# A graph-attention layer with a resident mask: eleven exponential tiles, the mask in nine pieces, the second mask quarter made before the main loop

## The chip, the cores and the metric

The kernel runs on one core of a Trainium2 chip. The metric is the device time of one execution in microseconds (us), the median of three runs. The core has a matrix engine (TensorE, PE in the profile; its weight loads are PEld), a vector engine (DVE), a scalar engine (ACT), GpSimd (POOL), a sync engine (SP) that here only issues transfers, and 16 DMA engines.

## The reference, cut to what matters

`x` is (8, 2048, 256) float32, `adj` is (2048, 2048) int32, one adjacency for all eight samples f. Heads: 8 of 32 channels.

```python
qkv = jnp.einsum('fnc,ck->fnk', x, w_qkv)
q, k, v = jnp.split(qkv, 3, axis=-1)            # then 8 heads of 32 channels
scores = jnp.einsum('fnhd,fmhd->fhnm', q, k) / jnp.sqrt(D)
scores = jnp.where((adj > 0)[None, None], scores, -1e9)
attn = jax.nn.softmax(scores, axis=-1)
t = jnp.einsum('fhnm,fmhd->fnhd', attn, v).reshape(F, N, C)
x = layernorm(x + t); x = layernorm(x + mlp(x)); x = layernorm(x0 + x)
```

## The kernel before

The 2048 queries of a sample are cut into four chunks `qc` of 512, the heads into two halves `g` of four heads, the keys into 16 blocks `mb` of 128. One **item** is (f, qc, g, mb); there are 8·4·2·16 = 1024 of them. The 16 items of one (f, qc, g) are called a **group** here and are numbered from 0 to 63, so that f = 0 is groups 0 to 7. An item makes scores for four heads (PE), adds the mask (DVE, two halves of 1024 columns), takes the exponential in place (ACT) and multiplies by V (PE). The sum of the exponentials is gathered in three chains, two by accumulating DMA and one on POOL, and finished by a matmul with ones (`denominator`).

The tiles that the change touches: `pp` holds the exponential tiles (8 KB a partition each), `mkp` the mask of one query chunk (16 blocks of 512 fp8 values, 8 KB a partition).

```python
mkp = ctx.enter_context(tc.tile_pool(name="mkp", bufs=2))
ld = ctx.enter_context(tc.tile_pool(name="ld", bufs=LD))          # LD = 3
pp = ctx.enter_context(tc.tile_pool(name="pp", bufs=10))
# ...
def scores(item):
    f, qc, g, mb = item
    pt = PT[item] = pp.tile([P, 4, CH], F32, name="p")
    ps2 = [score_pair() for _ in range(2)]
    # ... 4 matmuls into the two PSUM pairs (L223)
    for half, ps in enumerate(ps2):
        nc.vector.tensor_tensor(pt[:, 2 * half:2 * half + 2, :], ps,
                                MK[f, qc][:, mb, None, :].to_broadcast([P, 2, CH]), ALU.add)      # L226
    nc.scalar.activation(pt, pt, AF.Exp, scale=1.0 / math.sqrt(D))                                # L228

POOLED = (0, 3, 6, 8, 11, 13, 15)
MOVED = ((1, 4, 7, 10), (2, 5, 9, 12))
ALONE = 14

def add_up(item):
    f, qc, g, mb = item
    for chain in MOVED:
        if mb in chain[1:]:
            nc.gpsimd.dma_start(PT[f, qc, g, chain[0]], PT.pop(item), accum_op=ALU.add)           # L257
    if mb in POOLED[1:]:
        first = PT[f, qc, g, POOLED[0]]
        nc.gpsimd.tensor_tensor(first, first, PT.pop(item), ALU.add)                              # L260
```

A mask quarter is the mask of one query chunk. It is made once, during f = 0, from `adj`: a load, a conversion on DVE, 16 transposes of 128x128 per 512 keys on PE, and two copies out of PSUM on DVE. It is then stored in DRAM (`MD`) and loaded again for every other sample.

```python
def turn_mask(qc, mc):
    if mc == 0:
        MK[0, qc] = mkp.tile([P, MB, CH], F8, name="mask")
    yield INPUTS - 3
    cv = take([P, TPC, CH], BF16)
    ts = [take([P, 2, CH], I32) for _ in range(2)]
    for half, t in enumerate(ts):
        q0 = qc * CH + half * 2 * P
        nc.sync.dma_start(t, adj[q0:q0 + 2 * P, ...])                                             # L121
        nc.vector.tensor_scalar(cv[:, ...], t, 0.0, MASKED, op0=ALU.is_le, op1=ALU.mult)          # L122
        give(t)
        yield 1
    yield 1
    yield from mask_blocks(qc, mc, cv)      # transposes L136, copies L137; whole quarter stored, L140
    give(cv)

def load_mask(f, qc):
    MK[f, qc] = mkp.tile([P, MB, CH], F8, name="mask")
    nc.sync.dma_start(words(MK[f, qc]), MD[qc])                                                   # L144
```

`begin` runs before the main loop. It loads x and the adjacency of chunk 0 into the exponential tiles, makes K, V of the first head half and mask quarter 0, issues the scores of the first two items, and then makes K, V of the second head half:

```python
def begin():
    # ... loads, L427 and L428
    for c in range(NCK):
        nc.vector.tensor_scalar(cv[c], cols[c], 0.0, MASKED, op0=ALU.is_le, op1=ALU.mult)         # L431
        # ... turn rows, queries, project(0, c, 0)
        yield from mask_blocks(0, c, cv[c])
    for k in range(LEAD):                                                                         # LEAD = 2
        scores(items[k])
    for c in range(NCK):
        yield from project(0, c, 1, rows[c][:, 2:4, :])
```

The main loop walks the items in order. Everything else (masks, queries, projections of the next sample, the layer norms and the MLP, called the tail) stands in a list `fill`, sorted by due item; a `yield n` in it means that the next step is taken n items later at the earliest, and a step that needs a PSUM bank takes the one bank that each item has to spare.

```python
for t, (f, qc, g, mb) in enumerate(items):
    if f == 0 and g == 0 and mb == 0 and qc + 1 < NCK:
        start(t, mask_ahead(qc + 1), t + 28)
    if g == 1 and mb == 0 and (f or qc == NCK - 1) and (f + 1 < F or qc + 1 < NCK):
        load_mask(f + (qc + 1) // NCK, (qc + 1) % NCK)
    # ... work for the next sample is put into the list
    if mb:
        advance(t, 1)
    scores(items[t + LEAD])     # (cut: waits here until V of that item is made)
    values(items[t]); add_up(items[t])
    if mb == LAST:
        start(t + SUM, denominator(f, qc, g), t)
```

Of the kernel before, what the change touches and what calls it, by code (L numbers as in the profile page):

```python
# [30 lines left out]
MASKED = -57344.0  # L31
# [22 lines left out]
def fast_path(ctx, tc, cst, x, adj, out, RS):  # L54
    nc = tc.nc
    F, N, C = x.shape
    NCK, TPC, MB = N // CH, CH // P, N // P

    LD = 3
    dp = ctx.enter_context(tc.tile_pool(name="dp", bufs=1, space=bass.MemoryType.DRAM))  # L60
    mkp = ctx.enter_context(tc.tile_pool(name="mkp", bufs=2))
    ld = ctx.enter_context(tc.tile_pool(name="ld", bufs=LD))
    kp = ctx.enter_context(tc.tile_pool(name="kp", bufs=2 * NCK + 2))
    qp = ctx.enter_context(tc.tile_pool(name="qp", bufs=2 * NCK + 2))
    vp = ctx.enter_context(tc.tile_pool(name="vp", bufs=2 * NCK + 2))
    pp = ctx.enter_context(tc.tile_pool(name="pp", bufs=10))
    work = ctx.enter_context(tc.tile_pool(name="work", bufs=1))
    yp = ctx.enter_context(tc.tile_pool(name="yp", bufs=2))
    op = ctx.enter_context(tc.tile_pool(name="op", bufs=1))
# [28 lines left out]
    def take(shape, dt):  # L98
        live.pop(0)
        live.append(ld.tile(shape, dt, name="in"))  # L100
        return live[-1]

    def give(t):
        live[:] = [None if u is t else u for u in live]


    MD = dp.tile([NCK, P, MB * CH // 4], I32, name="md")
    MK = {}

    def words(mask):  # L110
        return mask.rearrange("p b q -> p (b q)").bitcast(I32)

    def turn_mask(qc, mc):
        if mc == 0:
            MK[0, qc] = mkp.tile([P, MB, CH], F8, name="mask")
        yield INPUTS - 3
        cv = take([P, TPC, CH], BF16)
        ts = [take([P, 2, CH], I32) for _ in range(2)]
        for half, t in enumerate(ts):
            q0 = qc * CH + half * 2 * P  # L120
            nc.sync.dma_start(t, adj[q0:q0 + 2 * P, mc * CH:(mc + 1) * CH].rearrange("(j p) m -> p j m", p=P))  # L121
            nc.vector.tensor_scalar(cv[:, 2 * half:2 * half + 2, :], t, 0.0, MASKED, op0=ALU.is_le, op1=ALU.mult)  # L122
            give(t)
            yield 1
        yield 1
        yield from mask_blocks(qc, mc, cv)
        give(cv)

    def mask_blocks(qc, mc, cv):
        for half in range(2):  # L130
            yield BANK
            ps = bank(BF16)
            for r in range(2):
                for j in range(TPC):
                    rr = 2 * half + r
                    nc.tensor.transpose(ps[:, r, j * P:(j + 1) * P], cv[:, j, rr * P:(rr + 1) * P], identb)  # L136
            nc.vector.tensor_tensor(MK[0, qc][:, mc * TPC + 2 * half:mc * TPC + 2 * half + 2, :], ps,  # L137
                                    cst["ones"][:, 0:1, None].to_broadcast([P, 2, CH]), ALU.min, saturate=False)
        if mc == NCK - 1:
            nc.sync.dma_start(MD[qc], words(MK[0, qc]))  # L140

    def load_mask(f, qc):
        MK[f, qc] = mkp.tile([P, MB, CH], F8, name="mask")
        nc.sync.dma_start(words(MK[f, qc]), MD[qc])  # L144


    QT, KT, V, XT = {}, {}, {}, {}
# [37 lines left out]
    def reload(f, c):  # L185
        while (f, c) not in XT:
            yield 1
        yield INPUTS - 1
        xT = take([P, 2, CH], F32)
        nc.sync.dma_start(xT, XD[f][c])  # L190
        yield 3
        return xT

    def project(f, c, g, xT=None):
        if xT is None:
            xT = yield from reload(f, c)
            while len(KT) < (2 * f + g) * NCK + c:
                yield 1
        yield BANK
        KT[f, c, g] = channels(kp, "kT", xT, C + g * P)  # L200
        yield BANK
        ps = bank()
        for j in range(TPC):
            for a in range(2):
                nc.tensor.matmul(ps[:, j * P:(j + 1) * P], xT[:, a, j * P:(j + 1) * P],  # L205
                                 wqkv[:, a, 2 * C + g * P:2 * C + (g + 1) * P], start=(a == 0), stop=(a == 1))
        v = vp.tile([P, TPC, P], F32, name="v")
        nc.scalar.copy(v, ps.rearrange("p (j c) -> p j c", c=P))
        V[f, c, g] = v
        give(xT)  # L210
# [9 lines left out]
        for half in (1, 0):  # L220
            for j in range(2):
                r = D * (2 * half + j)
                nc.tensor.matmul(ps2[half][:, j, :], KT[f, mb // TPC, g][r:r + D, (mb % TPC) * P:(mb % TPC + 1) * P],  # L223
                                 QT[f, qc, g][r:r + D, :], start=True, stop=True)
        for half, ps in enumerate(ps2):
            nc.vector.tensor_tensor(pt[:, 2 * half:2 * half + 2, :], ps,  # L226
                                    MK[f, qc][:, mb, None, :].to_broadcast([P, 2, CH]), ALU.add)
        nc.scalar.activation(pt, pt, AF.Exp, scale=1.0 / math.sqrt(D))  # L228

    LAST = MB - 1  # L230
# [149 lines left out]
    def start(t, gen, due):  # L380
        fill.append([t, gen, 1, due])
        fill.sort(key=lambda e: e[3])
# [24 lines left out]
    def mask_ahead(qc):  # L407
        for mc in range(NCK):
            yield from turn_mask(qc, mc)
# [9 lines left out]
    def begin():  # L419
        flat = [pp.tile([P, 4, CH], F32, name="p").rearrange("p a q -> p (a q)") for _ in range(NCK + NCK // 2)]  # L420
        cols = [t.bitcast(I32).rearrange("p (j m) -> p j m", m=CH) for t in flat[:NCK]]
        cv = [t[:, i * 2 * CH:(i + 1) * 2 * CH].bitcast(BF16).rearrange("p (j m) -> p j m", m=CH)
              for t in flat[NCK:] for i in range(2)]
        rows = [pp.tile([P, 4, CH], F32, name="p") for _ in range(NCK)]
        for c in range(NCK):
            xc = rows[c][:, 0:2, :].rearrange("p a (b c) -> p (a b) c", c=C)
            nc.sync.dma_start(xc, x[0, c * CH:(c + 1) * CH, :].rearrange("(j p) c -> p j c", p=P))  # L427
            nc.sync.dma_start(cols[c], adj[0:CH, c * CH:(c + 1) * CH].rearrange("(j p) m -> p j m", p=P))  # L428
        MK[0, 0] = mkp.tile([P, MB, CH], F8, name="mask")
        for c in range(NCK):  # L430
            nc.vector.tensor_scalar(cv[c], cols[c], 0.0, MASKED, op0=ALU.is_le, op1=ALU.mult)  # L431
            xT = rows[c][:, 2:4, :]
            yield from turn_rows(rows[c][:, 0:2, :].rearrange("p a (b c) -> p (a b) c", c=C), xT)
            nc.sync.dma_start(XD[0][c], xT)
            XT[0, c] = xT
            if c == 0:
                yield from queries(0, 0, xT)
            yield from project(0, c, 0, xT)
            yield from mask_blocks(0, c, cv[c])
        for k in range(LEAD):  # L440
            scores(items[k])
        for c in range(NCK):
            yield from project(0, c, 1, rows[c][:, 2:4, :])

    def ask(f, c):
        xT = yield from reload(f, c)
        yield from queries(f, c, xT)
        give(xT)

    for _ in begin():  # L450
        pass
    for c in range(1, NCK):
        start(0, ask(0, c), 2 * MB * c - LEAD - 1)
    state["side"] = 0
    for t, (f, qc, g, mb) in enumerate(items):
        if mb == 0 and t:
            state["side"] = 1 - state["side"]
        if f == 0 and g == 0 and mb == 0 and qc + 1 < NCK:
            start(t, mask_ahead(qc + 1), t + 28)
        if g == 1 and mb == 0 and (f or qc == NCK - 1) and (f + 1 < F or qc + 1 < NCK):  # L460
            load_mask(f + (qc + 1) // NCK, (qc + 1) % NCK)
        if f + 1 < F:
            for what, *which in NEXT.get((2 * qc + g, mb), []):
                due = t + MB // 2 if what is turn else items.index((f + 1, 0, which[1], which[0] * TPC)) - LEAD - 1
                start(t, what(f + 1, *which), due)
        if mb:
            advance(t, 1)
        if t + LEAD < len(items):
            nf, _, ng, nmb = items[t + LEAD]
            t0 = t  # L470
            while (nf, nmb // TPC, ng) not in V:
                advance(t0, 1)
                t0 += 1
            scores(items[t + LEAD])
        values(items[t])
        add_up(items[t])
        if mb == LAST:
            start(t + SUM, denominator(f, qc, g), t)
    t = len(items)
# [239 lines left out]
```

## Time and profile before

| what | value |
|---|---|
| time, median of 3 | 3736.42 us (3731.55 to 3740.82) |
| profiled span | 3732.1 us, mean granted TensorE clock 0.977 |
| busy: PE, DVE, POOL, ACT | 3241.8, 2760.8, 2599.1, 2411.0 us |
| mean DMA traffic | 154 GB/s, 573.31 MB |
| mask loads from DRAM | 28 of 1024 KB, 6.6 us to landing |

The page counts an engine as busy while an instruction of the program runs on it. A row of the groups names the line, the engine and the operation, then what it writes and reads, the count, the busy time and the mean duration, and the idle time of that engine just before such instructions with what ended it. In the list of waits a row "A <- B: s, n, m" says that A sat idle for B for s us in total, n times, m us at the longest. In a timeline a number in brackets is idle time just before the instruction. With 1024 items, an average item takes 3.6 us.

### The profile page before, as it was taken

What the parts mean: (1) busy time and instruction counts of PE and PEld (TensorE: products, weight loads), DVE (VectorE), ACT (ScalarE), POOL (GpSimd) and SP (SyncE); (2) the same over time, 40 slices, a digit from 0 to 9 for tenths busy, and PEclk for the clock granted to TensorE, in tenths of its full rate; (3) what the DMA queues carried; (4) which work ended last, traced back from release to release, by engine and by line L of the source; (5) the groups of instructions that cost most, each with busy time, mean ns of one, the idle gap of its engine ahead of it and who ended that gap; (6) DMA issues with size and microseconds to landing.
All of it is one profiled execution on the core that took longest, in us unless ns stands there. A gap on an engine that the chain in (4) does not pass through costs nothing. (4 is left out here: it accounts for less than half of the span.)

```text
span 3732.1 us, 53786 instructions
## 1 busy us (share of the span) xinstructions
PE 3241.8 (87%) x22020; PEld 1038.8 (28%) x22020; DVE 2760.8 (74%) x3203; ACT 2411.0 (65%) x1921; POOL 2599.1 (70%) x1363
## 2 busy tenths in 40 slices
PE   7877888899988899889998899889898889988884
PEld 4222223222322233222332223222232222322221
DVE  4777766877688766788677777777768877688883
ACT  3554555766667666766666776666666676677663
POOL 2555666777677775877667785777777777687775
PEclk9998999999999999999999999999999999999997
DMA  6766675776766775776766776676676676676664
GB/s 185 175 142 152 146 175 117 168 162 142 173 150 145 158 171 145 169 153 154 169 138 151 163 172 158 140 165 154 147 175 141 148 171 152 154 164 140 139 134 86
DMA packets 113774, 573.31 MB, mean 154 GB/s; under 512 B 10833, under 2 KB 27729, under 8 KB 60273
## 3 DMA queue, kind: packets, MB, share of 16 engines
q0 software_dynamic: 64848, 436.90, 58.1%
q1 hardware_dynamic: 47856, 131.61, 10.0%
q8 instruction: 174, 2.85, 0.3%
q10 hardware_dynamic: 816, 1.31, 0.1%
q14 instruction: 80, 0.65, 0.0%
HBM read 129.37 MB, written 37.75 MB: 45 GB/s over the span
## 5 line engine op out<-in xcount | busy, mean ns | idle before, releaser
L226 DVE TENSOR_TENSOR p<-s,mask 128x1024 f32<-128x1024 f32 x2048 | 2410.3, 1219 | 753.8 <-PE s L223 480.0
L228 ACT ACTIVATE p<-p 128x2048 f32<-128x2048 f32 x1024 | 1957.1, 1911 | 1232.9 <-DVE p L226 916.2
L260 POOL TENSOR_TENSOR p<-p 128x2048 f32<-128x2048 f32 x384 | 1835.9, 4810 | 653.6 <-ACT p L228 645.0
L223 PE MATMUL s<-qT,kT 32*128 32x512 f32 x8192 | 1193.2, 652 | 232.5 <-DVE p L226 231.0
L240 PE MATMUL x<-p,v 128*32 128x512 f32 x8192 | 1112.2, 616 | 0.0
L257 POOL DMA_DIRECT2D p<-p x384 | 382.7, 1018 | 351.2 <-ACT p L228 138.9
L223 PEld LDWEIGHTS s<-qT,kT 32*128 32x128 f32 x8192 | 325.3, 186 | 853.6 <-DVE p L226 695.6
L240 PEld LDWEIGHTS x<-p,v 128*32 128x32 f32 x8192 | 162.3, 108 | 795.2 <-issue 645.1
L180 PE MATMUL x<-in,wqkv 128*128 128x512 f32 x472 | 234.6, 620 | 23.1 <-ACT oT L244 10.2
L278 ACT ACTIVATE y<-y,nb,rs 128x256 f32<-128x256 f32 x384 | 224.9, 589 | 38.0 <-POOL nb L275 38.0
L294 PE MATMUL x<-p,ones 128*32 128x512 f32 x2048 | 246.3, 599 | 1.8 <-DVE y L364 0.9
L267 DVE BATCH_NORM_STATS2 st<-y 128x6 f32<-128x256 f32 x384 | 160.1, 417 | 27.1 <-DMA y<-in_x_dram 27.1
L362 PE MATMUL x<-w2s,hT 128*128 128x256 f32 x512 | 127.6, 392 | 45.7 <-ACT oT L244 42.3
L352 PE MATMUL x<-turned,w1s 128*128 128x512 f32 x256 | 128.8, 626 | 20.8 <-ACT hT L353 19.5
L180 PEld LDWEIGHTS x<-in,wqkv 128*128 128x128 f32 x472 | 80.3, 190 | 186.1 <-issue 69.8
L362 PEld LDWEIGHTS x<-w2s,hT 128*128 128x128 f32 x512 | 92.1, 190 | 112.0 <-ACT oT L244 68.6
L205 PE MATMUL x<-wqkv,in 128*128 128x128 f32 x896 | 114.9, 282 | 6.4 <-ACT kT L182 6.3
L205 PEld LDWEIGHTS x<-wqkv,in 128*128 128x128 f32 x896 | 104.2, 192 | 55.0 <-ACT kT L182 34.0
L364 DVE TENSOR_TENSOR y<-x,y 128x512 f32<-128x512 f32 x64 | 44.3, 692 | 94.9 <-PE x L362 94.7
L294 PEld LDWEIGHTS x<-p,ones 128*32 128x32 f32 x2048 | 64.0, 111 | 165.8 <-issue 129.7
L272 POOL TENSOR_TENSOR rs<-rs,mhalf 128x4 f32<-128x4 f32 x96 | 99.3, 1035 | 8.0
L341 PE MATMUL x<-ident,y 128*128 128x128 f32 x256 | 48.0, 299 | 54.5 <-ACT turned L342 38.8
(87 smaller groups left out, 1427.1 us busy)
## 6 DMA issues: line engine op xcount, KB each, us to landing
p<-p POOLq DMA_DIRECT2D x384, 1024.0 KB, 9.7
y<-in_x_dram POOLq DMA_DIRECT2D x64, 512.0 KB, 6.1
in<-xd SPq DMA_DIRECT2D x59, 512.0 KB, 8.0
mask<-md SPq DMA_DIRECT2D x28, 1024.0 KB, 6.6
out_dram<-y SPq DMA_DIRECT2D x32, 512.0 KB, 3.0
in<-in_x_dram SPq DMA_DIRECT2D x28, 512.0 KB, 6.9
xd<-in SPq DMA_DIRECT2D x28, 512.0 KB, 10.0
in<-in_adj_dram SPq DMA_DIRECT2D x24, 512.0 KB, 7.6
```

The source lines that it names most:

```text
L180: nc.tensor.matmul(ps, wqkv[:, a, k0:k0 + P], xT[:, a, :], start=(a == 0), stop=(a == 1))
L205: nc.tensor.matmul(ps[:, j * P:(j + 1) * P], xT[:, a, j * P:(j + 1) * P], wqkv[:, a, 2 * C + g * P:2 * C + (g + 1) * P], start=(a == 0), s ...
L223: nc.tensor.matmul(ps2[half][:, j, :], KT[f, mb // TPC, g][r:r + D, (mb % TPC) * P:(mb % TPC + 1) * P], QT[f, qc, g][r:r + D, :], start=Tr ...
L226: nc.vector.tensor_tensor(pt[:, 2 * half:2 * half + 2, :], ps, MK[f, qc][:, mb, None, :].to_broadcast([P, 2, CH]), ALU.add)
L228: nc.scalar.activation(pt, pt, AF.Exp, scale=1.0 / math.sqrt(D))
L240: nc.tensor.matmul(O[grp][r:r + D, :], V[f, mb // TPC, g][:, mb % TPC, r:r + D], PT[item][:, h, :], start=(mb == 0), stop=(mb == LAST))
L257: nc.gpsimd.dma_start(PT[f, qc, g, chain[0]], PT.pop(item), accum_op=ALU.add)
L260: nc.gpsimd.tensor_tensor(first, first, PT.pop(item), ALU.add)
L267: nc.vector.bn_stats(st, t[:, j, :])
L278: nc.scalar.activation(t[:, j, :], t[:, j, :], AF.Identity, bias=nb[:, j:j + 1], scale=rs[:, j:j + 1])
L294: nc.tensor.matmul(ps[r:r + D, :], cst["ones"], term[:, h, :], start=(n == 0), stop=(n == 3))
L362: nc.tensor.matmul(ps[:, (j - jj) * C:(j - jj + 1) * C], hT[:, d, j * P:(j + 1) * P], w2s[:, d, :], start=(d == 0), stop=(d == 1))
```

## The change

The two whole mask buffers (16 KB a partition) become nine pieces of two key blocks (1 KB each, 9 KB together); the room goes to an eleventh exponential tile. A sample's mask is loaded piece by piece: while the second head half of one query chunk runs, at every second item one piece of the next chunk's mask is loaded, each as soon as it has been made. During f = 0 the quarters 1 to 3 are also loaded back from DRAM instead of being built in place: what the copies out of PSUM write is a staging place in the load buffers, and from there it is stored. The two loads and the two conversions of a step of `turn_mask` are set apart by two items. Mask quarter 1 is made in `begin`, beside K and V of the second head half, with exponential tiles as load buffers; quarters 2 and 3 start at items 16 and 32.

```diff
-    mkp = ctx.enter_context(tc.tile_pool(name="mkp", bufs=2))
+    mkp = ctx.enter_context(tc.tile_pool(name="mkp", bufs=MB // 2 + 1))
-    pp = ctx.enter_context(tc.tile_pool(name="pp", bufs=10))
+    pp = ctx.enter_context(tc.tile_pool(name="pp", bufs=11))
...
     def turn_mask(qc, mc):
-        if mc == 0:
-            MK[0, qc] = mkp.tile([P, MB, CH], F8, name="mask")
         yield INPUTS - 3
...
             nc.sync.dma_start(t, adj[q0:q0 + 2 * P, mc * CH:(mc + 1) * CH].rearrange("(j p) m -> p j m", p=P))
+        yield 2
+        for half, t in enumerate(ts):
             nc.vector.tensor_scalar(cv[:, 2 * half:2 * half + 2, :], t, 0.0, MASKED, op0=ALU.is_le, op1=ALU.mult)
-            give(t)
-            yield 1
-        yield 1
-        yield from mask_blocks(qc, mc, cv)
+        yield 1
+        yield from mask_blocks(qc, mc, cv, [... the two load buffers, seen as fp8 ...])
+        for t in ts:
+            give(t)
         give(cv)
...
-            nc.vector.tensor_tensor(MK[0, qc][:, ...], ps, ..., ALU.min, saturate=False)
-        if mc == NCK - 1:
-            nc.sync.dma_start(MD[qc], words(MK[0, qc]))
+            k = 2 * mc + half
+            m = to[half] if to else mask_piece(0, qc, k)
+            nc.vector.tensor_tensor(m, ps, ..., ALU.min, saturate=False)
+            nc.sync.dma_start(MD[qc, k], words(m))
+            made.add((qc, k))
-    def load_mask(f, qc):
-        MK[f, qc] = mkp.tile([P, MB, CH], F8, name="mask")
-        nc.sync.dma_start(words(MK[f, qc]), MD[qc])
+    def load_mask(f, qc, k):
+        nc.sync.dma_start(words(mask_piece(f, qc, k)), MD[qc, k])
...
         for c in range(NCK):                                    # in begin
+            t = pp.tile([P, 4, CH], F32, name="p").rearrange("p a q -> p (a q)")
+            col = t.bitcast(I32).rearrange("p (j m) -> p j m", m=CH)
+            nc.sync.dma_start(col, adj[CH:2 * CH, c * CH:(c + 1) * CH].rearrange("(j p) m -> p j m", p=P))
+            nc.vector.tensor_scalar(cv[c], col, 0.0, MASKED, op0=ALU.is_le, op1=ALU.mult)
             yield from project(0, c, 1, rows[c][:, 2:4, :])
+            yield from mask_blocks(1, c, cv[c], [... two parts of t, seen as fp8 ...])
...
     for c in range(1, NCK):
         start(0, ask(0, c), 2 * MB * c - LEAD - 1)
+        if c > 1:
+            start(MB * (c - 1), mask_ahead(c), 2 * MB * c - MB // 2)
...
-        if f == 0 and g == 0 and mb == 0 and qc + 1 < NCK:
-            start(t, mask_ahead(qc + 1), t + 28)
-        if g == 1 and mb == 0 and (f or qc == NCK - 1) and (f + 1 < F or qc + 1 < NCK):
-            load_mask(f + (qc + 1) // NCK, (qc + 1) % NCK)
+        if g == 1 and mb % 2 and (f + 1 < F or qc + 1 < NCK):
+            coming.append((f + (qc + 1) // NCK, (qc + 1) % NCK, mb // 2))
+        while coming and coming[0][1:] in made:
+            load_mask(*coming.popleft())
```

More of the change, by code (lines that the diff above doesn't have):

```diff
@@ L104, in give, with mask_piece @@
         live[:] = [None if u is t else u for u in live]
-    MD = dp.tile([NCK, P, MB * CH // 4], I32, name="md")
+    MD = dp.tile([NCK, MB // 2, P, 2 * CH // 4], I32, name="md")
     MK = {}
+    made, coming = set(), deque()
     def words(mask):
         return mask.rearrange("p b q -> p (b q)").bitcast(I32)
+    def mask_piece(t, qc, k):
+        MK[t, qc, k] = mkp.tile([P, 2, CH], F8, name="mask")
+        return MK[t, qc, k]
     def turn_mask(qc, mc):
-        if mc == 0:
-            MK[0, qc] = mkp.tile([P, MB, CH], F8, name="mask")
         yield INPUTS - 3
@@ L121, in turn_mask, with mask_blocks @@
             nc.sync.dma_start(t, adj[q0:q0 + 2 * P, mc * CH:(mc + 1) * CH].rearrange("(j p) m -> p j m", p=P))
+        yield 2
+        for half, t in enumerate(ts):
             nc.vector.tensor_scalar(cv[:, 2 * half:2 * half + 2, :], t, 0.0, MASKED, op0=ALU.is_le, op1=ALU.mult)
+        yield 1
+        yield from mask_blocks(qc, mc, cv, [t.rearrange("p j m -> p (j m)").bitcast(F8)[:, 0:2 * CH].rearrange("p (b q) -> p b q", q=CH)
+                                            for t in ts])
+        for t in ts:
             give(t)
-            yield 1
-        yield 1
-        yield from mask_blocks(qc, mc, cv)
         give(cv)
-    def mask_blocks(qc, mc, cv):
+    def mask_blocks(qc, mc, cv, to=None):
         for half in range(2):
@@ L136, in mask_blocks @@
                     nc.tensor.transpose(ps[:, r, j * P:(j + 1) * P], cv[:, j, rr * P:(rr + 1) * P], identb)
-            nc.vector.tensor_tensor(MK[0, qc][:, mc * TPC + 2 * half:mc * TPC + 2 * half + 2, :], ps,
-                                    cst["ones"][:, 0:1, None].to_broadcast([P, 2, CH]), ALU.min, saturate=False)
-        if mc == NCK - 1:
-            nc.sync.dma_start(MD[qc], words(MK[0, qc]))
-    def load_mask(f, qc):
-        MK[f, qc] = mkp.tile([P, MB, CH], F8, name="mask")
-        nc.sync.dma_start(words(MK[f, qc]), MD[qc])
+            k = 2 * mc + half
+            m = to[half] if to else mask_piece(0, qc, k)
+            nc.vector.tensor_tensor(m, ps, cst["ones"][:, 0:1, None].to_broadcast([P, 2, CH]), ALU.min, saturate=False)
+            nc.sync.dma_start(MD[qc, k], words(m))
+            made.add((qc, k))
+    def load_mask(f, qc, k):
+        nc.sync.dma_start(words(mask_piece(f, qc, k)), MD[qc, k])
     QT, KT, V, XT = {}, {}, {}, {}
@@ L226, in scores @@
             nc.vector.tensor_tensor(pt[:, 2 * half:2 * half + 2, :], ps,
-                                    MK[f, qc][:, mb, None, :].to_broadcast([P, 2, CH]), ALU.add)
+                                    MK[f, qc, mb // 2][:, mb % 2, None, :].to_broadcast([P, 2, CH]), ALU.add)
         nc.scalar.activation(pt, pt, AF.Exp, scale=1.0 / math.sqrt(D))
@@ L428, in begin @@
             nc.sync.dma_start(cols[c], adj[0:CH, c * CH:(c + 1) * CH].rearrange("(j p) m -> p j m", p=P))
-        MK[0, 0] = mkp.tile([P, MB, CH], F8, name="mask")
         for c in range(NCK):
@@ L442, in begin @@
         for c in range(NCK):
+            t = pp.tile([P, 4, CH], F32, name="p").rearrange("p a q -> p (a q)")
+            col = t.bitcast(I32).rearrange("p (j m) -> p j m", m=CH)
+            nc.sync.dma_start(col, adj[CH:2 * CH, c * CH:(c + 1) * CH].rearrange("(j p) m -> p j m", p=P))
+            nc.vector.tensor_scalar(cv[c], col, 0.0, MASKED, op0=ALU.is_le, op1=ALU.mult)
             yield from project(0, c, 1, rows[c][:, 2:4, :])
+            yield from mask_blocks(1, c, cv[c], [t[:, i * CH // 2:(i + 1) * CH // 2].bitcast(F8).rearrange("p (b q) -> p b q", q=CH)
+                                                 for i in range(2)])
     def ask(f, c):
```

## The prediction

> **What bounds the kernel now.** I read the page's busy table first.
>
> ```profile
> PE 3241.8 (87%) x22020; PEld 1038.8 (28%) x22020; DVE 2760.8 (74%) x3203; ACT 2411.0 (65%) x1921; POOL 2599.1 (70%) x1363
> ```
>
> TensorE is busy for 87% of the span and nothing else comes near. The change removes no score, value or projection, so it can win only idle time of PE: 3732 - 3242 = 490 us at the very most. Where does it lie? I cut the span at the first value matmul of each sample (start of the loop at 58 us, its end at 3664) and asked for the table by stage. Columns: window, its length, busy PE, PEld, DVE, ACT, POOL, then clock, DMA share, GB/s.
>
> ```profile
> 0.00:58.00 58.00, 47.13 (x292) 31.83 (x296) 19.32 (x18) 19.82 (x29) 6.75 (x19) 1.00 0.64 215
> 58.00:568.00 510.00, 412.36 (x2760) 125.96 (x2756) 378.40 (x391) 282.59 (x207) 297.87 (x135) 0.93 0.67 154
> 568.00:1031.00 463.00, 414.52 (x2804) 137.33 (x2800) 336.80 (x395) 306.37 (x253) 325.53 (x172) 0.99 0.70 157
> 1031.00:1474.00 443.00, 396.96 (x2716) 126.45 (x2712) 335.62 (x392) 300.53 (x240) 323.98 (x168) 1.00 0.71 157
> ```
>
> Sample 0, which makes the masks, takes 510 us with 98 of them idle on PE; sample 1 takes 463; sample 2 and the four after it 443 to 448, with some 46 idle. Sample 0 is thus 65 us, sample 1 about 18 us longer than a settled one. The 18 sit in its first group alone, 69 us against 52 in a later sample:
>
> ```profile
> 568.00:637.00 69.00, 60.35 (x408) 24.00 (x404) 42.93 (x51) 39.69 (x36) 42.12 (x24) 0.98 0.67 153
> 1474.00:1526.00 52.00, 44.66 (x332) 13.63 (x324) 42.71 (x49) 34.51 (x24) 32.10 (x18) 0.98 0.65 135
> ```
>
> PE has 16 us more work there: projections for which sample 0 found no free bank in time. So the masks cost time where they are made, and again as a backlog.
>
> Then the waits of DVE that the change touches, in the list of waits:
>
> ```profile
> DVE in L122 <- DMA in<-in_adj_dram: 35.6, 8, 8.6
> ...
> DVE p L226 <- DMA p<-p: 25.8, 19, 5.0
> ```
>
> The first is the adjacency load that is issued and converted in one step. The timeline at 280 us shows what one costs: issued at 280.45, converted at 283.16, and PE stood still for 7.23 us, because the scores' PSUM pairs were not emptied:
>
> ```profile
> 283.16 0.69 DVE L122 TENSOR_SCALAR in<-in 128x1024 bf16<-128x1024 int32 x1 [8.64 <-DMA in<-in_adj_dram]
> ...
> 285.04 2.09 PE L223 MATMUL s<-qT,kT 32*128 32x512 f32 x8 [7.23 <-DVE p L226]
> ```
>
> The matmuls after it took 2.09 us for 1.14, so a stop costs a little more than its length. The second wait is the exponential tile: all ten are taken, and the next is free only when an accumulating DMA has read it. Seen at 1523 us, in the second item of a group:
>
> ```profile
> 1522.93 2.36 DVE L226 TENSOR_TENSOR p<-s,mask 128x1024 f32<-128x1024 f32 x2 [1.46 <-DMA p<-p]
> ```
>
> **What the Trainium skill says.** "SBUF — State Buffer", section "SBUF: two separate sides": DVE and GpSimd share one port pair as an exclusive lock, so one blocks for the whole of the other's instruction. The trace agrees: a conversion (L122) has a median of 0.685 us and took 5.56 us at 214.72, while a POOL addition ran from 214.93 for 4.80 us. Before the loop POOL does no such additions; conversions moved there are safe. "DMA: Bandwidth & Descriptors", section "Anatomy of one DMA — SWDGE (gpsimd) path": a wait sits on the issuing sequencer before dispatch, so transfers that one engine issues stand in a line. The trace agrees: SP spends 1736 us in total at the xT store (L171) until ACT has made xT, and what it issues later stands behind that. "Perfetto Trace Analysis", section "DMA Optimizations": transfers under 2 KB carry a large overhead. This would speak against 1 KB pieces, but the packets of the hardware queue in this trace took 50 ns for 1 KB and 365 for 8 KB, the same per byte; the measurement decides, and I charge the pieces nothing.
>
> **Part 1, eleven tiles.** In the built program the tile taken by the second item of a group is that of the item 7 before (the tenth of the last group, end of a DMA chain); with eleven tiles it is that of the item 8 before. Put against the times of this trace, the new previous users would be done at least 2.7 us before their tile is wanted in samples 1 to 7 (the old ones: 0.1 us, and late in 23 cases). So the wait goes. Of the 25.8 us about 5 lie in one stop in sample 0; from 568 us on there are 19.3 us in 17 waits. A stopped item takes 4.0 to 4.4 us where an unstopped one in the same place takes 2.83, and the next sometimes 0.7 more: 15 stops of weight at 1.2 to 1.9 us is 18 to 28. I take **-22**.
>
> **Part 2, conversions set apart from loads.** A load lands in 7.6 us (page, median); two items are about 7. Of the 35.6 us, 9.3 belong to quarter 1 (counted in part 3), 26.3 to quarters 2 and 3. I leave 8 of those and get 18, of which group 3 (243 to 314 us) alone has 15.2 and is just 15 us longer than in later samples. Blocked conversions of some 5 us remain for quarters 2 and 3.
>
> **Part 3, quarter 1 leaves the loop.** Its 64 transposes at 0.084 us are 5.4 us of PE; its 8 conversions and 8 copies 8 x 0.685 + 8 x 1.22 = 15.2 us of DVE, with 9.3 of waits. Group 0 is 12.5 us longer than later first groups. But the query projections of sample 0's other three chunks (six tiles of two 512-wide matmuls, about 1 us each by L180: 255 us for 256) now stand in group 0 instead of group 1 in the built program. I count groups 0 and 1 together: 63.5 + 59.2 become 57 + 51, **-14**. Part 2 and the one tile stop make -13 more in groups 2 to 7 (-10 of it in group 3; elsewhere work that now comes earlier fills what is freed), so sample 0 changes by **-27**. By the built program the backlog of group 8 falls to a single projection (8 of its 128x128 matmuls for 40, no 512-wide ones for 8), 16 us of PE work, which goes into groups 5 to 7, whose idle time and freed stops take it: **-18** for sample 1.
>
> **Part 4, what quarter 1 costs before the loop.** Now the price. From 41 to 57 us PE works and DVE is nearly free:
>
> ```profile
> 41.00:57.00 16.00, 15.76 (x92) 10.89 (x96) 3.68 (x4) 8.02 (x10) 0.00 (x0) 1.00 0.30 93
> ```
>
> It looks like a good home: 15 us of DVE work would fit. But the order on SP in the built program is load column 0, store two pieces, load column 1, and so on. The stores wait for the copies out of PSUM, so the next column's load cannot be issued before the last one is finished. One round is: load 1 MB about 5.5 us (the same size as the mask loads' 6.6 and the mask stores' 4.9), conversion 1.23 (L431), transposes 0.6 until the first bank, two copies 2.44, issues and semaphores about 1: 10.8 us. Four rounds from 39.2 us end at 82; the projections (3.5 us each) run inside them. The first value matmul moves from 57.7 to about 81: **+24**.
>
> **Sum.** -22 - 27 - 18 + 24 = -43: 3736 - 43 = 3693.
>
> **Rivals.** (a) *The serial rounds hide*: SP could run ahead, or loads land in 4 us; then part 4 is +10 to +18 and the time 3675 to 3685. Against it: the store stands between the loads on the same queue. (b) *The tile is not the limit*: groups whose second item waits for PE instead take 4.0 us as well (first groups of a sample); then part 1 brings 5 instead of 22 and the time is 3710. For it speaks that 511 of DVE's waits at L226 (480.0 us) are for PE; against it, groups 13, 21, 29, where no tile was late, take 2.83. (c) *The pieces get late*: 248 loads of 128 KB for 28 of 1 MB go through SP, each waiting for DVE to leave its slot, and SP cannot run as far ahead with x and xT loads. A piece is asked for about 13 items (45 us) before use against some 7 us to land, so I hold it unlikely; if it failed, every group would lose a us or two, 3736 to 3790. (d) *Sample 0 heals more than I count*: its clock is 0.93 against 1.00, so with fewer stops its 412 us of PE shrink as well; up to -30 more, 3660.
>
> **Range and chances.** Parts 1 to 3 have an uncertainty of about 8, 15 and 8 us, part 4 of 6; (c) adds a tail above, (d) one below. So 3655 to 3725. 2% is 75 us, a time below 3662: it needs nearly all of (a) and (d), 0.10. Slower by 2% needs (c) in full, 0.02. Within 2%: 0.88.
>
> **What would show it.** Right: first value matmul near 81 us, with PE idle for some 6 us between projections and transposes; no DVE wait for "DMA p<-p" after sample 0; sample 0 near 483 us; group 8 near 51; samples 2 to 6 at about 3 us less each; waits for in_adj in the loop under 10 us. Wrong: a start of 60 to 70 us (a), samples 2 to 6 unchanged (b), a DVE wait for "DMA mask<-md" (c).

## The result, and the profile after

| | before | after |
|---|---|---|
| time, median of 4 | 3733.99 us | 3709.51 us (3708.02 to 3710.73) |
| ratio | | 0.9933, interval 0.9915 to 0.9951 |
| profiled span | 3732.1 us | 3706.2 us |

The change makes the kernel 0.7% faster (a fourth run moved the median before from 3736.42 to 3733.99 us). The prediction was 3693 us with a range of 3655 to 3725, so the total is in the range, but it is the sum of parts of which one went the other way. The stages show it. This is the table by stage of the changed kernel, cut at the first value matmul of the loop and of each sample (columns as before: window, length, busy PE, PEld, DVE, ACT, POOL, clock, DMA share, GB/s):

```profile
0.00:84.00 84.00, 59.98 (x352) 39.79 (x352) 33.22 (x29) 19.95 (x29) 7.49 (x19) 0.88 0.59 199
84.00:595.00 511.00, 414.70 (x2774) 130.22 (x2772) 361.34 (x376) 288.02 (x218) 298.33 (x139) 0.93 0.67 156
595.00:1037.00 442.00, 396.45 (x2728) 126.51 (x2728) 336.32 (x393) 300.66 (x240) 324.49 (x168) 1.00 0.72 158
1037.00:1479.00 442.00, 397.58 (x2726) 126.91 (x2728) 335.93 (x392) 300.68 (x241) 324.54 (x168) 1.00 0.71 158
```

With the exact starts of the first value matmuls instead of whole microseconds:

| stage | before | after | change | predicted |
|---|---|---|---|---|
| up to the first value matmul | 57.7 | 84.4 | +26.7 | +24 |
| sample 0 (makes the masks) | 509.9 | 510.9 | +1.0 | -27 |
| sample 1 | 463.1 | 441.6 | -21.5 | -18 |
| samples 2 to 7 | 2633.2 | 2600.0 | -33.2 | -22 (with a little of sample 1) |
| after the last value matmul | 68.2 | 69.3 | +1.1 | 0 |

Three parts came out near what was predicted or better. Sample 0 did not gain at all, although its first group fell from 63.5 to 50.8 us: group 2 rose from 62.6 to 74.2. In the list of waits, the wait for the exponential tile is nearly gone, and the wait for the adjacency (35.6 us before), which the change was to shorten, has grown, though it now covers 16 loads instead of 24:

```profile
DVE in L127 <- DMA in<-in_adj_dram: 44.3, 8, 9.9
...
DVE p L233 <- DMA p<-p: 1.7, 3, 0.8
```

The longest of them in the timeline: two loads are issued at 229.86, DVE is ready for the data at 230.5, and TensorE, whose transposes stand behind the conversion, lost 9.59 us:

```profile
229.86 1.72 SPq L124 DMA_DIRECT2D in<-in_adj_dram  x2
...
240.43 0.69 DVE L127 TENSOR_SCALAR in<-in 128x1024 bf16<-128x1024 int32 x1 [9.90 <-DMA in<-in_adj_dram]
241.18 0.39 PE L143 MATMUL x<-identb,in 128*128 128x128 bf16 x2 [9.59 <-DVE in L127]
```

The load itself took 10.1 us, and the second of the pair 18.4, among accumulating transfers that took 10.7 to 12.6 each. Before the loop, with no accumulating transfer under way, the loads of quarter 1, 1 MB each, landed in 4.9 to 5.3 us. And the load was issued only 0.7 us before DVE wanted it.

### The profile page after: what moved, and what is told of

Same layout as the page of the kernel before. It is cut to its first block, busy times and chain, and to the rows that moved or that the text cites. A ratio compares the mean times of both kernels' runs of the same rounds, so it can differ in the third digit from the quotient of the medians.

```text
span 3706.2 us, 54441 instructions
## 1 busy us (share of the span) xinstructions
PE 3218.3 (87%) x22020; PEld 1038.1 (28%) x22020; DVE 2755.5 (74%) x3199; ACT 2410.3 (65%) x1921; POOL 2602.4 (70%) x1363
## 3 DMA queue, kind: packets, MB, share of 16 engines
q1 hardware_dynamic: 83504, 134.77, 10.8%
## 5 line engine op out<-in xcount | busy, mean ns | idle before, releaser
L230 PE MATMUL s<-qT,kT 32*128 32x512 f32 x8192 | 1179.2, 644 | 173.0 <-DVE p L233 171.5
L247 PE MATMUL x<-p,v 128*32 128x512 f32 x8192 | 1097.5, 608 | 0.0
L371 DVE TENSOR_TENSOR y<-x,y 128x512 f32<-128x512 f32 x64 | 44.3, 692 | 100.2 <-ACT p L235 62.3
```

The lines of the kernel that those rows point to most:

```text
L247: nc.tensor.matmul(O[grp][r:r + D, :], V[f, mb // TPC, g][:, mb % TPC, r:r + D], PT[item][:, h, :], start=(mb == 0), stop=(mb == LAST))
```

## The experiments

Each ran against the kernel before on the same chip; a ratio is to that kernel, whose median was 3734 to 3743 us from chip to chip, so runs are best compared by ratio and by stage. The stages are those of the profiled run.

| run | time | ratio, interval | start | sample 0 | sample 1 | samples 2 to 7 |
|---|---|---|---|---|---|---|
| before | 3733.99 | 1 | 57.7 | 509.9 | 463.1 | 2633.2 |
| after | 3709.51 | 0.9933 (0.9915 to 0.9951) | 84.4 | 510.9 | 441.6 | 2600.0 |
| s1_ahead | 3696.89 | 0.9887 (0.9870 to 0.9904) | 70.7 | 508.0 | 441.4 | 2602.6 |
| s3_far6 | 3700.24 | 0.9896 (0.9879 to 0.9914) | 88.1 | 478.0 | 460.8 | 2600.1 |
| s5_ten | 3744.05 | 1.0012 (1.0005 to 1.0019) | 87.6 | 513.6 | 444.1 | 2629.9 |
| b2_q1begin | 3717.97 | 0.9938 (0.9921 to 0.9955) | 67.8 | 485.8 | 464.1 | 2630.8 |
| s4_stage | 3713.86 | 0.9935 (0.9909 to 0.9961) | 87.9 | 508.4 | 440.7 | 2603.5 |
| s2_nosplit | 3752.67 | 1.0033 (1.0025 to 1.0042) | 89.1 | 551.3 | 440.5 | 2603.2 |
| b1_split | 3744.55 | 1.0014 (1.0005 to 1.0023) | 64.8 | 513.3 | 464.4 | 2633.1 |
| s7_combo | 3675.79 | 0.9827 (0.9801 to 0.9853) | 72.2 | 482.1 | 454.4 | 2600.2 |
| a1_split_act | 3717.52 | 0.9954 (0.9937 to 0.9972) | 61.6 | 490.7 | 463.3 | 2633.3 |
| a3_after_act | 3714.16 | 0.9942 (0.9923 to 0.9961) | 87.3 | 507.0 | 440.9 | 2603.6 |
| a2_combo_act | 3671.43 | 0.9829 (0.9812 to 0.9847) | 69.6 | 473.7 | 454.0 | 2606.4 |
| a4_stage_pool | 3689.51 | 0.9855 (0.9831 to 0.9879) | 89.0 | 482.4 | 440.2 | 2601.6 |

The start varies between runs of the same beginning: 84.4 to 89.1 us in the seven kernels that begin like the changed one, 57.7 to 64.8 in the three that begin like the kernel before. Most of this lies ahead of the first score matmul, which starts at 36.7 to 41.3 us, with the landing of the first adjacency load (15.0 to 19.2 us). Counted from the first score matmul to the first value matmul, the stretch takes 20.9 us before (22.5 and 24.0 in the other two) and 47.7 after (46.2 to 49.1 in the seven).

### The eleventh tile (s5_ten)

```diff
-    pp = ctx.enter_context(tc.tile_pool(name="pp", bufs=11))
+    pp = ctx.enter_context(tc.tile_pool(name="pp", bufs=10))
```

> The changed kernel with ten exponential tiles instead of eleven. Theory 3 (the eleventh tile is what samples 2 to 7 won, 33 us): DVE waits for accumulating transfers come back in the second item of groups 1 and 3 of a sample, about 20 us of them; samples 2 to 7 together return from 2600 to 2630 us, the time is about 3735 to 3745. Rival (the mask in pieces, without bursts of 1 MB, is what won it): samples 2 to 7 stay within 5 us of 2600; about 3712.

Samples 2 to 7 returned to 2629.9 us, and the wait came back:

```profile
DVE p L233 <- DMA p<-p: 19.9, 22, 1.7
```

So the eleventh tile is worth 30 us there and 2.5 in sample 1, more than the 22 predicted, and the mask in pieces brings at most the 3 us by which s5_ten stays below the kernel before. Without the tile the rest of the change is a small loss: 1.0012. In the changed kernel the second item of group 25, which had stopped DVE for 1.46 us, starts with no idle time before it (second row):

```profile
1522.87 2.36 DVE L233 TENSOR_TENSOR p<-s,mask 128x1024 f32<-128x1024 f32 x2 [0.20 <-PE s L230]
...
1525.70 2.35 DVE L233 TENSOR_TENSOR p<-s,mask 128x1024 f32<-128x1024 f32 x2
```

### The start: a store between two loads (s1_ahead, b2_q1begin)

The serial rounds are plain in the timeline of the changed kernel: the store (L147), the next load (L451), 5 us later the conversion, and TensorE idle 5.36 us for it, then copies and the next store.

```profile
52.32 0.43 SPq L451 DMA_DIRECT2D p<-in_adj_dram  x1
...
57.60 1.23 DVE L452 TENSOR_SCALAR p<-p 128x2048 bf16<-128x2048 int32 x1 [5.68 <-DMA p<-in_adj_dram]
58.89 1.04 PE L143 MATMUL s<-identb,p 128*128 128x128 bf16 x8 [5.36 <-DVE p L452]
...
61.21 1.45 SPq L147 DMA_DIRECT2D md<-p  x2
62.71 0.43 SPq L451 DMA_DIRECT2D p<-in_adj_dram  x1
```

A round takes 62.71 - 52.32 = 10.4 us; the prediction had 10.8. s1_ahead issues the load of the next column first:

```diff
+        def column(c):                        # tile and load of column c
...
+        ahead = [column(0)]
         for c in range(NCK):
+            if c + 1 < NCK:
+                ahead.append(column(c + 1))       # its load is issued here
+            t, col = ahead[c]
             nc.vector.tensor_scalar(cv[c], col, 0.0, MASKED, op0=ALU.is_le, op1=ALU.mult)
```

> The changed kernel, with one alteration: before the loop, the load of the next column of quarter 1 is issued ahead of the stores of the column before. Theory 1 (the serial round load, conversion, transposes, copies, store, next load sets the 84.4 us at which the first value matmul starts): it starts at 60 to 66 us, and the time falls from 3709 by 18 to 24 to about 3688. Rival (DVE or PE work itself fills the stretch before the loop, or what starts earlier waits later for the same transfers): the start stays above 75 us, or it falls and sample 0 grows by as much; 3700 to 3710.

The start came to 70.7 us, above the 60 to 66 expected, but theory 1 holds. Counted from the first score matmul the stretch falls from 47.7 to 30.7 us, by 17.0; the start itself shows only 13.7 of it, since this run's first scores came 3.2 us later. The time fell by as much, from 0.9933 to 0.9887 of the kernel before. What is left is mostly work: TensorE is busy for 26.6 us of this stretch, against 18.7 in the kernel before; from 46.5 us on its longest gap is 1.00 us; and from 44 to 50 us its granted clock was 0.50, where four 512-wide projection matmuls took 3.78 us for 1.98.

b2_q1begin makes quarter 1 before the loop in the kernel before, straight into the mask buffer, with one store at the end:

```diff
+        MK[0, 1] = mkp.tile([P, MB, CH], F8, name="mask")
         for c in range(NCK):
+            # ... column c loaded and converted, as in the change
             yield from project(0, c, 1, rows[c][:, 2:4, :])
+            yield from mask_blocks(1, c, cv[c])
...
-        if f == 0 and g == 0 and mb == 0 and qc + 1 < NCK:
+        if f == 0 and g == 0 and mb == 0 and 0 < qc < NCK - 1:
```

> The kernel before, with one part of the change alone: mask quarter 1 is made before the loop, straight into the second mask buffer, and stored once at its end, so that no store stands between two column loads. By theory 1 the start grows only by the PE work, from 57.7 to 62 to 68 us; group 0 loses its 12 us, the backlog in the first group of sample 1 shrinks from 69 towards 51 us: 3736 falls to 3705 to 3715. Rival (what is freed in group 0 is lost again in groups 1 to 4, as in the changed kernel): only the start grows and sample 0 keeps 505 or more; 3735 to 3745.

It costs 10.1 us at the start (7.6 from the first score matmul) and frees 24.1 in sample 0: groups 0 and 1 take 98.9 us for 122.7. The move itself is good; of its price of 27 us in the changed kernel 17 are the store in the line. One part of the expectation was wrong: the first group of sample 1 still takes 69.8 us, and so the time, 3718.0, stays above the range expected. TensorE has 96 projection matmuls to do in that group, as many as in the kernel before; in the changed kernel it has 16. So it was not quarter 1 leaving the loop that removed the backlog; in the changed kernel quarters 2 and 3 also start earlier, at items 16 and 32 for 32 and 64, which was not run alone. The earlier start seems to have its price: two of the four steps of quarter 2 now fall into group 1, which takes 60.9 us in the changed kernel and 48.3 in b2_q1begin.

### Why sample 0 gained nothing (s3_far6, s2_nosplit, s4_stage, a4_stage_pool)

```diff
 # s3_far6
-        yield 2
+        yield 6
 # s2_nosplit
-        yield 2
         for half, t in enumerate(ts):
             nc.vector.tensor_scalar(cv[:, 2 * half:2 * half + 2, :], t, ...)
+            yield 1
```

> The changed kernel with six items instead of two between the loads of an adjacency step and their conversions. Theory 2 (two items, some 6 us, are too short for a load that takes 10 to 24 us among the accumulating transfers, so DVE still stands still): waits of DVE for the adjacency in the loop fall from 44.3 us to below 10, sample 0 from 511 to about 475, the time to 3675 to 3685. Rival (the load buffers that are held longer delay the projections of the next sample, which come back as a backlog in sample 1, or the store of the pieces delays the loads by as much): sample 0 above 495 or sample 1 above 450; 3700 to 3715.

> The changed kernel with each conversion directly behind the two loads of its step, as before the change, all else kept. If the two items between load and conversion do what they were meant for, the waits of DVE for the adjacency rise from 44 us by some 6 us for each of the eight steps, to 70 to 95 us, and sample 0 from 511 to 525 to 545. Rival (the two items are lost to late issue and change nothing): waits of 40 to 55 us, sample 0 within 6 us of 511; time about 3710.

With six items the waits fall to 8.5 us and sample 0 to 478.0 us, as theory 2 says; the rival is right too, since sample 1 rises to 460.8: its first two groups have 128 projection matmuls to do, in the changed kernel 24. That the load buffers are held longer is the likely reason; it was not shown. With no distance, each conversion directly behind its own load, the waits are 77.5 us and sample 0 takes 551.3. So the two items do help in the new order. But the kernel before had no distance either, and there quarters 2 and 3 waited only 26.3 us. Something else had become worse. s4_stage and a4_stage_pool look for it:

```diff
 # s4_stage
-    mkp = ctx.enter_context(tc.tile_pool(name="mkp", bufs=MB // 2 + 1))
+    mkp = ctx.enter_context(tc.tile_pool(name="mkp", bufs=MB // 2))
+    stg = ctx.enter_context(tc.tile_pool(name="stg", bufs=2))
...
             nc.vector.tensor_scalar(cv[:, 2 * half:2 * half + 2, :], t, ...)
+            give(t)
...
-        yield from mask_blocks(qc, mc, cv, [... the load buffers ...])
+        yield from mask_blocks(qc, mc, cv, stg)
 # a4_stage_pool, on top of it
-            nc.sync.dma_start(MD[qc, k], words(m))
+            (nc.gpsimd if to is stg else nc.sync).dma_start(MD[qc, k], words(m))
```

> The changed kernel with two small staging tiles of its own for the mask pieces (and eight mask pieces instead of nine, to make room), so that a load buffer is free as soon as it is converted and the next load need not wait until a stored piece has landed. The order on TensorE stays that of the changed kernel. Theory 2a (the load is issued late because of the store's landing): the waits of DVE for the adjacency fall from 44 to below 25 us, group 2 from 74 to below 66 us, sample 0 by 10 to 20 us. Theory 2b (the load itself is slow among the accumulating transfers, 10 to 24 us, whenever it is issued): the waits stay above 35 us and sample 0 within 5 us of 511.

> The changed kernel with staging tiles of its own, as in the run of that alone, and the stores of the mask pieces of the loop issued by GpSimd instead of SP, so that no store stands between two adjacency loads on one queue. Theory 5 (the stores took SP's run ahead: before the change a load was issued 12.9 us before DVE wanted it, in the changed kernel 7.1, with own staging alone 8.5, against a landing of 8 to 10): the lead rises to 11 us or more, the waits of DVE for the adjacency fall from 40 to below 25 us, sample 0 from 508 to 485 to 498. Rival (the lead is set by the buffers or by the mask pieces on SP): lead below 10 us, waits above 33, sample 0 within 6 us of 508.

Own staging changed next to nothing (waits 40.5 us, sample 0 508.4): the store's landing is not the cause. Moving the stores off SP's queue changed much: sample 0 fell to 482.4 us, with sample 1 at 440.2, and the waits to 18.1. The conversions of that run (shortest, median and longest in ns; then the idle time of DVE before them in us):

```profile
L128 DVE TENSOR_SCALAR in<-in x16: 661/688/5003, 174.7 to 369.1; 128x1024 bf16<-128x1024 int32 x16
...
  issue: 9.8, 1
  DMA in<-in_adj_dram: 8.3, 3
```

The idle time of 9.8 us that the view puts down to "issue" ended 0.1 us after the load of that conversion had landed, so it belongs to the load as well.

The measure is how long before DVE wanted it a load was issued (start of the conversion, less the idle time before it, less the issue; mean of the 16 loads of quarters 2 and 3), against its landing time:

| run | lead | landing | waits |
|---|---|---|---|
| before | 12.9 us | 8.4 us | 26.3 us |
| after | 7.1 | 9.1 | 44.3 |
| s2_nosplit | 3.1 | 7.8 | 81.9, 4.4 of it under "issue" |
| s4_stage | 8.5 | 10.3 | 40.5 |
| s3_far6 | 18.9 | 8.5 | 8.5 |
| a4_stage_pool | 16.8 | 10.9 | 18.1, 9.8 of it under "issue" |

These are means of a wide spread. Before the change five of the 16 leads were over 19 us and eight under 7; after it the longest is 17.5 and nine are under 7; in a4_stage_pool none is under 9.5.

Before the change SP reached a load early and waited there only for its buffer to come free, 158 us in all from 120 to 530 us. Afterwards the stores of the mask pieces stand in its line, and each waits for DVE's copies, which are made just before the next load is due:

```profile
199.80 3.71 SPq L147 DMA_DIRECT2D md<-in  x2
203.56 0.98 SPq L124 DMA_DIRECT2D in<-in_adj_dram  x2
222.36 3.73 SPq L147 DMA_DIRECT2D md<-in  x2
229.86 1.72 SPq L124 DMA_DIRECT2D in<-in_adj_dram  x2
```

At the adjacency loads themselves SP now waits for only 13 us; in a4_stage_pool it is 70 again. The waits of SP in the changed kernel from 135 to 595 us:

```profile
SPq L147 <- DVE in L146: 142.6, 16, 23.6
SPq L151 <- DVE p L233: 110.5, 15, 34.6
```

The first row is those stores. The second, the mask pieces, is longer in a4_stage_pool (243.0 us), and the loads keep their lead all the same.

Two things stay open. In a4_stage_pool it is GpSimd that waits for the copies (53.0 us), which also moves its additions and the accumulating transfers that it issues; what part of the gain of 26 us over s4_stage comes from that was not separated. And both loads of a step are issued together since the change: the second landed in 10.8 us on average, the first in 7.4. This was not run alone.

### The wait that turned into a slow conversion (b1_split, a1_split_act)

b1_split puts the two items between loads and conversions into the kernel before, alone.

```diff
             nc.sync.dma_start(t, adj[q0:q0 + 2 * P, ...])
+        yield 2
+        for half, t in enumerate(ts):
             nc.vector.tensor_scalar(cv[:, 2 * half:2 * half + 2, :], t, ...)
             give(t)
-            yield 1
         yield 1
```

> The kernel before with one part alone: both loads of an adjacency step first, two items later both conversions. Masks are still built in place, so a load never waits for a store. By my prediction's part 2 the waits for the adjacency fall from 35.6 us to about 12, sample 0 from 510 to 485 to 495. By theory 2b (slow loads) the waits fall less, to 20 to 30 us, and sample 0 to 498 to 508. In both, samples 2 to 7 stay at 2630.

Both expectations were wrong. The waits did fall, from 35.6 to 9.1 us, and nothing came of it: sample 0 takes 513.3 us, for 509.9. The gain went into the conversions. First the row of the groups before, then that of b1_split (busy time and mean ns, then idle time before):

```profile
L122 DVE TENSOR_SCALAR in<-in 128x1024 bf16<-128x1024 int32 x24 | 32.0, 1333 | 35.6 <-DMA in<-in_adj_dram 35.6
```

```profile
L124 DVE TENSOR_SCALAR in<-in 128x1024 bf16<-128x1024 int32 x24 | 61.2, 2581 | 10.7 <-DMA in<-in_adj_dram 9.1 <-issue 1.5
```

Waits and conversions together: 35.6 + 32.0 = 67.6 us before, 9.1 + 61.2 = 70.3 here. In the timeline of b1_split two conversions take 13.22 us where they need 1.4, while POOL goes from one tensor operation to the next:

```profile
362.93 4.86 POOL L261 TENSOR_TENSOR p<-p 128x2048 f32<-128x2048 f32 x1
365.08 13.22 DVE L124 TENSOR_SCALAR in<-in 128x1024 bf16<-128x1024 int32 x2
...
368.50 2.51 POOL L368 TENSOR_TENSOR y<-y,g2r 128x1024 f32<-128x1024 f32 x1
370.80 4.65 POOL L261 TENSOR_TENSOR p<-p 128x2048 f32<-128x2048 f32 x1
375.25 2.49 POOL L370 TENSOR_TENSOR y<-y,be2r 128x1024 f32<-128x1024 f32 x1
```

They end at 378.3, POOL's run at 377.7. This is the exclusive lock on the shared ports that "SBUF — State Buffer" of the Trainium skill describes in "SBUF: two separate sides". The whole run agrees: 12 of its 24 conversions took over 1 us, each of them overlaps a tensor operation of POOL and ended 0.5 to 0.6 us after one; the 12 others took 0.7 us and overlap none. Before the change 5 of 24 took over 1 us.

After a long wait a conversion is quick: of the eight that had waited for more than 6 us in the kernels before and after, seven took 0.69 us, and six of the eight met no operation of POOL. But coming in time does not by itself make it slow: the mean was 2.2 us in s3_far6 and s7_combo and only 1.23 in a4_stage_pool, where the waits had fallen too. Why the conversions meet POOL so often in b1_split is not shown. a1_split_act takes the conversion off DVE:

```diff
-            nc.vector.tensor_scalar(cv[:, ...], t, 0.0, MASKED, op0=ALU.is_le, op1=ALU.mult)
+            nc.scalar.activation(cv[:, ...], t, AF.Identity, bias=cst["masked"], scale=-MASKED)
... (and the constant that it adds)
```

> The kernel before with loads and conversions two items apart, as in the run of that alone, and the conversion moved from DVE to the scalar engine (57344 a - 57344, which is right for an adjacency of 0 and 1 as here, not for other values). Theory 4 (with the load's wait gone, the conversion meets POOL's additions, which hold the port pair it needs, and takes 2.6 us on average for 0.7): the 61 us of conversions leave DVE, on the scalar engine each takes about 1 us and none over 3; sample 0 falls from 513 to 470 to 490, the time from 3745 to 3705 to 3725. Rival (it is TensorE's order, transposes waiting for the conversion wherever it runs): TensorE's waits for the conversion stay at 30 us or more and sample 0 above 500.

On ACT every conversion takes 1.13 us:

```profile
L124 ACT ACTIVATE in<-in,masked 128x1024 bf16<-128x1024 int32 x24 | 26.4, 1135 | 11.3 <-DMA in<-in_adj_dram 11.3
```

Sample 0 falls to 490.7 us, a shade above what theory 4 allowed, and the time from 3744.6 to 3717.5. TensorE's wait for the conversion fell from 34.9 to 19.3 us and did not go away. So the lock is what swallowed the gain of b1_split, or most of it; the move also takes the conversions' own 16 us off DVE, which was not separated.

In the changed kernel the same move should bring little, since there the load is what is late:

> The changed kernel with the conversions of the loop on the scalar engine (57344 a - 57344, right for an adjacency of 0 and 1). If the load's slowness alone is what stops DVE there (two items apart are too few), the stop moves to the scalar engine, which then waits some 40 us for the adjacency, and sample 0 stays within 10 us of 511. If the blocked conversions are a part of it (21.9 us in 16), sample 0 falls by 10 to 20 us.

It does: sample 0 takes 507.0 us for 510.9, and ACT now waits 39.7 us for the adjacency; the times do not differ.

### Versions put together (s7_combo, a2_combo_act)

```diff
 # on top of s1_ahead
-        yield 2
+        yield 4
...
-            start(MB * (c - 1), mask_ahead(c), 2 * MB * c - MB // 2)
+            start(8 if c == 2 else 24, mask_ahead(c), 2 * MB * c - 24)
```

> A version that puts together what the first runs showed: the changed kernel, next column's load ahead of the stores before the loop, four items between load and conversion, and quarters 2 and 3 starting at items 8 and 24 with a due time 16 items earlier, so that less of the next sample's projections is left for group 8. Start about 70 us, waits for the adjacency 10 to 25 us, sample 0 480 to 490, sample 1 445 to 458: 3675 to 3690. Rival (the backlog of sample 1 takes all that sample 0 gains): 3695 to 3705.

> The best version so far (next column ahead of the stores, four items between load and conversion, quarters 2 and 3 started at items 8 and 24) with the conversions of the loop on the scalar engine (right for an adjacency of 0 and 1). By theory 4 the 34 us of conversions on DVE become 16 on the scalar engine and TensorE's 27 us of waits for them fall below 12: sample 0 from 482 to 462 to 472, the time from 3676 to 3656 to 3668. Rival (DVE had slack there): within 6 us of 3676.

s7_combo takes 3675.8 us, 1.7% below the kernel before, and computes the same as that kernel for every adjacency. All its stages lie where they were expected (start, sample 0, sample 1), and DVE's waits for the adjacency are 11.1 us:

```profile
0.00:72.00 72.00, 55.01 (x352) 37.75 (x352) 33.14 (x29) 19.93 (x29) 6.75 (x19) 0.93 0.71 230
72.00:554.00 482.00, 401.15 (x2710) 122.33 (x2708) 373.80 (x376) 283.31 (x208) 300.01 (x139) 0.95 0.71 162
554.00:1009.00 455.00, 411.57 (x2792) 135.15 (x2792) 336.58 (x394) 305.55 (x251) 324.22 (x168) 1.00 0.71 157
```

With its conversions on ACT (a2_combo_act) sample 0 takes 8 us less (473.7 us), but the intervals of the two times overlap, and the expectation failed: TensorE's waits for the conversion fell from 27.2 only to 24.5 us, and 3671.4 is within the 6 us of the rival. Stores off SP's queue and the next column ahead together were not tried.

## Why the prediction was right, and where not

- **Part 1, eleven tiles, -22: right in cause, too small.** s5_ten gives 32, which is 1.5 us for each of its 22 waits: the cost of a stop was right, and the term that was mis-sized is their number, 15. Against the kernel before, which has 17 such waits from sample 1 on, the last sample stands out, with 12.8 us won for four waits; why is not shown.
- **Part 2, conversions set apart, the step that failed.** "I leave 8 of those" became 44.3. I treated a load as issued in the same step as its conversion, so that two items would add 7 us to nothing. But before the change SP already ran ahead and issued the loads 12.9 us before they were wanted, and the new stores took that away: with the two items the lead is 7.1 us, and with the stores on another queue 16.8. My example was misread for the same reason: the conversion at 283.16 did not wait for the load of 280.45 but for one issued at 269.45, which took 13.6 us; that of 280.45 landed at 292.6. I had the sentence that transfers of one engine stand in a line and applied it to the loads before the loop only. I also took the median landing, 7.6 us, for every load: five of the eight loads that DVE waited for, with 33 of the 44 us, landed in 10 to 24. And even where the wait does fall, in b1_split, the gain goes into the conversions: 45 us of blocking in 24 of them, where I had left some 5 for quarters 2 and 3.
- **Part 3, quarter 1 leaves the loop: right in the sum of the first two groups, partly by luck.** Groups 0 and 1 took 111.7 us for 122.7, -11 where I had -14. But b2_q1begin shows that quarter 1 alone is worth -24 there; the two steps of quarter 2 that moved into group 1, which I had not counted there, are the likely reason that half of it is missing. Groups 2 to 7 rose by 12.1 us (387.2 to 399.3) where I had -13; that is mainly part 2, whose waits grew by 18. Sample 1 fell as predicted, by 21.5, with some 2.5 of it the tile's, and group 8 took 49.2 us, near the 51 of the prediction.
- **Part 4, the price before the loop, +24: right** in size and cause. It was +26.7, rounds of 10.4 us; s1_ahead takes 17 of it back with the order of issue alone.
- **The rivals.** (a) and (b) fell. (c) named the right weakness, that SP can no longer run ahead, with the wrong victims: mask pieces are never late for DVE, the adjacency is. Nor does the remark on transfers under 2 KB bear on the pieces: a piece is one transfer of 128 KB, and only its packets are 1 KB. (d) fell: sample 0's clock stayed at 0.93.

In the sum, sample 0 was 28 us worse than thought and samples 1 to 7 some 15 better, so the total lies in the range in part because two misses have opposite signs.

## What to carry to other kernels

Before a transfer is put on a queue, ask what stands ahead of it there and what that waits for: a store that waits for a computed result takes away the run ahead that hid the loads behind it. Size the distance between a load and its use by the slow landings in that stage, not by the median of the page. When a wait is taken away, look at how long the instruction behind it then takes: here 26.5 us of waiting came back as 29.2 us of longer conversions, blocked by another engine.

## What the runs showed of the hardware that was not expected

- The same DVE conversion took 0.66 to 10.02 us, depending on what POOL did; its mean was 1.33, 2.58 and 1.39 us in before, b1_split and after.
- In the changed kernel a load of 512 KB landed in 4.1 to 5.0 us with no 1 MB accumulating transfer under way and in up to 24.4 among several, which took 10 to 14 us each then.
- Stores of the mask, 128 KB each: all eight of quarter 1, before the loop, landed in 1.7 us, ten of the 16 in the loop too, and the other six in up to 8.9.
